# Stating the first two blocks of a lane's next image ahead of the other lane's Fourier and bilinear blocks

## The chip, the cores and the metric

The kernel runs on one core of a Trainium2 chip. It is measured by the device time of one execution in microseconds, as the median of several runs. It is written for a tile framework with a scheduler: the Python code states operations, the framework works out which of them depend on each other, and a scheduler that goes through a simulated timeline fixes, while the program is built, the order in which each engine will execute its own instructions. Where several instructions could go next on an engine, the one stated earlier is preferred. On the chip each engine follows its fixed order, and waits on semaphores for the results of the others.

## The reference

The input x holds 16 images of 56 x 56 positions with 128 channels, in float32. Each image goes through four blocks, each added to its own input:

```python
x = x + L0(_gn(x), ...)   # attention inside shifted 7 x 7 windows, 4 heads
x = x + L1(_gn(x), ...)   # triangle: gated projections, einsum over rows, layer norms
x = x + L2(_gn(x), ...)   # Fourier operators, attention over 56 "time" rows, 32 heads
x = x + L3(_gn(x), ...)   # q, k, v; depthwise 3 x 7 convolutions; three bilinear products
```

Here `_gn` is a group norm with 32 groups of 4 channels. In the Fourier block an image is read as 56 planes of 56 x 128: spectral convolutions that keep a few modes give queries, keys and values, the planes attend to each other, and two more Fourier operators with a GELU between them follow. In the bilinear block

```python
kernel = einsum('xnk,xkd->xnd', q, K_H1)
feature = einsum('xvw,xvd->xwd', V_G, feature)
out = einsum('xnd,xvd->xvn', kernel, feature)
```

is computed at each of the 3,136 positions of an image. Images don't depend on each other.

## The kernel before

An image lies in on-chip memory as 128 channels by 3,136 positions (`xt`). `load_image` (L433) brings it in with 7 loads on SyncE's queue (SP, L439), each followed by 4 transposes on TensorE. Then the four blocks run on it: `_window_attention` (L480), `_triangle` (L615), `_fourier` (L729), `_bilinear` (L1276). The bilinear block writes the result itself, chunk by chunk (L1445), so `store_image` isn't used.

There are two lanes. Image b belongs to lane b % 2, and each lane has its own buffers: one large work area (`arena`, 128 x 17,152 floats), 5 small work tiles (`w2`), 8 tiny ones, 4 banks of PSUM (two single ones, `psb`, and a double one, `psd`), 12 DRAM buffers (`dy`). Each block takes its lane's arena for itself, so inside a lane the blocks run strictly one after the other. The images are in a pool of two buffers that both lanes share, so the next image of a lane can be loaded only once the image before it in the same lane is done. What overlaps is therefore always one image of lane 0 with one image of lane 1.

The blocks differ in what they use. The first two are made of many small matmuls and the evictions of their results, and move almost no data. The Fourier block has an early part (norms, column transforms, attention weights, with the wide products of L1093), a loop over a table (L1188 to L1226: 128 transfers issued by GpSimd at L1200, each read of a table from DRAM multiplied by VectorE at L1202 and summed by TensorE), and a late part (inverse transforms and two operators, with GpSimd clearing buffers at L973, L974 and L1250). The bilinear block writes each of 21 intermediate results to DRAM eight times over (`dy`, L1314, on ScalarE's queue), reads them back spread over the partitions (84 transfers of 448 KB per image, L1408, on SP's queue), multiplies them on VectorE (L1411) and sums the products on TensorE (the helper `together`, L368 and L371).

The order of statements is a plain loop over the images: all four blocks of image 0, then all four of image 1, and so on. So at every moment the scheduler prefers the lane with the older image.

Of the kernel before, what the change touches and what calls it, by code (L numbers as in the profile page):

```python
# [307 lines left out]
def tile_blocks(ctx: ExitStack, tc: tile.TileContext, ins, out, at, stages=(0, 1, 2, 3)):  # L308
    nc = tc.nc
    x_in = ins["x"]  # L310
    NB = x_in.shape[0]
# [16 lines left out]
    lane = [0]  # L328
    count = [0]

    def uid(s):
        count[0] += 1
        return f"{s}{count[0]}"
# [4 lines left out]
    def w2():  # L338
        return w2p[lane[0]].tile([P, 512], F32, tag="w2", name=uid("w2_"))
# [4 lines left out]
    def psb():  # L344
        return ps1[lane[0]].tile([P, 512], F32, tag="ps1", name=uid("psb"))
# [37 lines left out]
    def W(name):  # L383
        rows, o, n = at["wgt"][name]
        return wgt[:rows, o : o + n]
# [47 lines left out]
    def load_image(b):  # L433

        xt = xpool.tile([P, NTOK], F32, tag="xt", name=uid("xt"))
        for q in range(NCH):
            t = w2()
            tv = t[:TT, :].rearrange("p (a c) -> p a c", a=4)
            nc.sync.dma_start(  # L439
                out=tv,  # L440
                in_=xf[b, q * CH : (q + 1) * CH, :].rearrange("(a p) c -> p a c", p=TT),
            )
            p = psb()
            for a in range(4):
                nc.tensor.transpose(p[:, a * TT : (a + 1) * TT], tv[:, a, :], ident[:TT, :TT])
            act(xt[:, q * CH : (q + 1) * CH], p[:, :CH], AF.Identity, bias=W("bout0"))
        return xt

    def store_image(b, xt):
        for q in range(NCH):  # L450
            p = psb()
            for a in range(4):
                o = q * CH + a * TT
                nc.tensor.transpose(p[:TT, a * P : (a + 1) * P], xt[:, o : o + TT], ident)
            t = w2()
            nc.scalar.copy(t[:TT, :], p[:TT, :])
            nc.sync.dma_start(
                out=of[b, q * CH : (q + 1) * CH, :].rearrange("(a p) c -> p a c", p=TT),
                in_=t[:TT, :].rearrange("p (a c) -> p a c", a=4),
            )  # L460
# [1 line left out]
    env = dict(locals())  # L462
    blocks = [_window_attention, _triangle, _fourier, _bilinear]
    run = {s: blocks[s](env) for s in stages}
    for b in range(NB):
        lane[0] = b % 2
        xt = load_image(b)
        done = False
        for s in stages:
            done = run[s](b, xt)  # L470
        if not done:
            store_image(b, xt)


class _Env:
# [1008 lines left out]
def _build(inputs, bacc, stages=(0, 1, 2, 3)):  # L1484
    x = np.ascontiguousarray(inputs["x"])
    w, early, late = _weights({k: v for k, v in inputs.items() if k != "x"})
    arrays, at = {"x": x}, {}
    for name, parts in (("cst", _constants()), ("wgt", w), ("early", early), ("late", late)):
        arrays[name], at[name] = _pack(parts)
    nc = bacc.Bacc("TRN2", target_bir_lowering=False, num_devices=1)  # L1490
    ins = {k: nc.dram_tensor(k, v.shape, F32, kind="ExternalInput").ap() for k, v in arrays.items()}
    out = nc.dram_tensor("out", x.shape, F32, kind="ExternalOutput").ap()
    with tile.TileContext(nc, schedule_with_timeline_sim=True) as tc:
        tile_blocks(tc, ins, out, at, stages)
    return nc, arrays, out, at
```

## Time and profile before

| | |
|---|---|
| runs | 13,435.75, 13,443.8 and 13,488.92 us; median 13,443.8 us |
| profiled execution | 13,405.75 us; span in the profile 13,403.8 us |
| mean TensorE clock granted | 0.847 |
| moved by DMA | 2,106 MB, 157 GB/s over the span |

The profile of this page comes from one execution. Its busy shares say how much of the span an engine executed something. PE is TensorE, PEld its weight loads, DVE is VectorE, ACT ScalarE, POOL GpSimd, SP the queue of SyncE. The three numbers of a wait are the total in us, how often, and the longest. The two costliest groups are the multiplications of the bilinear block and of the table loop, both on VectorE:

```profile
L1411 DVE TENSOR_TENSOR arena<-arena 128x1792 f32<-128x1792 f32 x1344 | 2661.8, 2018 | 724.6 <-DMA arena<-dy 329.5
L1202 DVE TENSOR_TENSOR arena<-arena 112x1344 f32<-112x1344 f32 x1024 | 1569.5, 1552 | 356.8 <-DMA arena<-table 341.1
```

Such a line reads: line and engine, operation, what is written and read with shapes, how many; then busy time and mean nanoseconds of one; then the idle time of the engine ahead of these, and what ended most of it. Since every instruction of an engine stands in the built program in the order in which it runs, the records of VectorE can be paired one by one with the program, and so be told apart by image and block. One image keeps VectorE busy for 82.5 us in the window attention, 67.5 in the triangle, 275 in the Fourier block and 212.5 in the bilinear block.

### The profile page before, as it was taken

How to read it: one execution, taken by the hardware profiler on the slowest of the kernel's cores; microseconds unless marked ns; L12 is line 12 of the kernel's file. 1: busy time of each engine (PE TensorE's matmuls, PEld its weight loads, DVE VectorE, ACT ScalarE, POOL GpSimd, SP SyncE). 2: the span in 40 equal slices, each digit the busy share in tenths (PEclk: the TensorE clock that was granted, in tenths of full speed). 3: DMA queues.
4: the chain of work that ended last, by engine and by line, in shares of the span. 5: the costliest groups of instructions: out<-in, count | busy, mean ns of one | idle time of the engine just before them, and what ended most of it. 6: DMA issues, size and time to landing. Idle time of an engine off the chain costs nothing. (4 is left out here: it accounts for less than half of the span.)

```text
span 13403.8 us, 202422 instructions
## 1 busy us (share of the span) xinstructions
PE 10585.8 (79%) x82624; PEld 5860.7 (44%) x82624; DVE 9623.6 (72%) x13985; ACT 3845.7 (29%) x6638; POOL 1426.4 (11%) x2746
## 2 busy tenths in 40 slices
PE   7887687876878778887778877888778887788776
PEld 4454254542544335443355433554335443354432
DVE  7776868667677686676766667767777677866776
ACT  3223141321423224232242222422224232242221
POOL 0120002200022000220002200022000220002200
PEclk9988898878988889888888778888888888888887
DMA  1256904468044680447804468044780447704577
GB/s 35 73 164 230 315 1 118 118 244 300 1 124 124 237 294 9 118 138 240 276 10 118 131 228 291 13 118 130 245 279 10 118 136 252 270 7 118 131 249 267
DMA packets 1091758, 2105.94 MB, mean 157 GB/s; under 512 B 98320, under 2 KB 974096, under 8 KB 1089680
## 3 DMA queue, kind: packets, MB, share of 16 engines
q1 hardware_dynamic: 560000, 823.95, 18.7%
q0 software_dynamic: 165120, 629.61, 17.1%
q10 hardware_dynamic: 365712, 639.44, 13.2%
q8 instruction: 654, 10.72, 0.3%
q14 instruction: 272, 2.23, 0.1%
HBM read 1412.73 MB, written 667.03 MB: 155 GB/s over the span
## 5 line engine op out<-in xcount | busy, mean ns | idle before, releaser
L1411 DVE TENSOR_TENSOR arena<-arena 128x1792 f32<-128x1792 f32 x1344 | 2661.8, 2018 | 724.6 <-DMA arena<-dy 329.5
L1202 DVE TENSOR_TENSOR arena<-arena 112x1344 f32<-112x1344 f32 x1024 | 1569.5, 1552 | 356.8 <-DMA arena<-table 341.1
L371 PE MATMUL psb<-arena,cst 128*32 128x448 f32 x9792 | 1578.0, 672 | 0.0
L368 PE MATMUL psb<-arena,cst 128*32 128x448 f32 x1408 | 818.8, 670 | 799.9 <-DVE arena L1411 750.3
L1200 POOL DMA_DIRECT2D arena<-table x2048 | 1063.7, 521 | 2799.3 <-PE psb L1116 724.8
L371 PE MATMUL psb<-arena 112*64 112x224 f32 (+2 forms) x4864 | 1245.2, 525 | 0.0
L368 PE MATMUL psb<-arena 112*64 112x448 f32 (+1 forms) x1280 | 691.4, 625 | 369.2 <-DVE arena L1093 187.5
L371 PE MATMUL psd<-arena 112*64 112x224 f32 (+1 forms) x3072 | 749.4, 465 | 0.0
L368 PE MATMUL psd<-arena 112*64 112x448 f32 x1024 | 554.5, 627 | 211.4 <-DVE arena L1202 190.9
L1093 DVE TENSOR_TENSOR arena<-w,coef 128x1792 f32<-128x1792 f32 x256 | 507.6, 2020 | 210.7 <-PE psb L371 187.4
L371 PEld LDWEIGHTS psb<-arena 112*64 112x64 f32 (+1 forms) x4864 | 435.6, 153 | 509.7 <-issue 507.3
L368 PEld LDWEIGHTS psb<-arena,cst 128*32 128x32 f32 x1408 | 118.4, 119 | 1154.3 <-DVE arena L1411 869.2
L678 PE MATMUL psd<-wgt,arena 128*64 128x128 f32 x7168 | 514.4, 293 | 112.4 <-DVE arena L690 96.5
L371 PEld LDWEIGHTS psb<-arena,cst 128*32 128x32 f32 x9792 | 367.6, 125 | 471.4 <-issue 451.0
L1396 ACT COPY arena<-psd 128x896 f32<-128x896 f32 x336 | 303.4, 905 | 930.8 <-DVE arena L1411 549.4
L678 PEld LDWEIGHTS psd<-wgt,arena 128*64 128x64 f32 x7168 | 450.0, 145 | 217.1 <-issue 129.2
L907 PE MATMUL psb<-cst,arena 128*128 128x64 f32 (+1 forms) x2688 | 454.9, 341 | 92.4 <-ACT arena L917 63.2
L371 PE MATMUL psd<-arena,wgt 128*32 128x448 f32 x2688 | 500.6, 604 | 34.4 <-DMA arena<-padded 34.0
L907 PEld LDWEIGHTS psb<-cst,arena 128*128 128x128 f32 x2688 | 437.2, 254 | 148.8 <-ACT arena L917 74.0
L1313 ACT COPY w<-psb 128x448 f32<-128x448 f32 x336 | 178.6, 532 | 1089.1 <-PE psb L371 761.8
L368 PE MATMUL psd<-arena,wgt 128*32 128x448 f32 x896 | 438.6, 607 | 42.4 <-DMA arena<-padded 37.4
L371 PEld LDWEIGHTS psd<-arena 112*64 112x64 f32 x3072 | 287.0, 151 | 284.4 <-issue 283.0
(299 smaller groups left out, 19594.2 us busy)
## 6 DMA issues: line engine op xcount, KB each, us to landing
arena<-table POOLq DMA_DIRECT2D x2048, 294.0 KB, 8.7
dy<-w ACTq DMA_DIRECT2D x336, 1792.0 KB
arena<-dy SPq DMA_DIRECT2D x1344, 448.0 KB
arena<-padded SPq DMA_DIRECT2D x896, 162.8 KB
w<-x SPq DMA_DIRECT2D x112, 224.0 KB
out<-w SPq DMA_DIRECT2D x112, 224.0 KB
padded<-w ACTq DMA_DIRECT2D x336, 62.0 KB
arena<-arena POOLq DMA_DIRECT2D x16, 784.0 KB, 9.8
```

The source lines that it names most:

```text
L368: done = mm(**first)
L371: mm(**kw)
L678: mm(p[half : half + 64, i // 4, i % 4 * P : (i % 4 + 1) * P], lhsT=xh[:, c0 : c0 + 64], rhs=W(w).rearrange("p (k c) -> p k c", c=64)[:, : ...
L907: mm(p[:, 2 * i * nl : 2 * (i + 1) * nl], lhsT=src[:, t * P : (t + 1) * P], rhs=fc, start=True, stop=True)
L1093: tt(t4, bc(ys[c][:, l0 : l0 + 4, :], 1, 8), bc(coef[:, c, h0 : h0 + 8, l0 : l0 + 4], 3, T), ALU.mult,)
L1200: nc.gpsimd.dma_start(out=t[hh * T : (hh + 1) * T, :], in_=bc(tflat[q, two, hh], 0, T))
L1202: tt(t4, bc(x3[:, :, s], 1, 2), t4, ALU.mult)
L1313: nc.scalar.copy(t[:, :CH], p[:, :CH])
L1396: nc.scalar.copy(z, p[:, :, :CH])
L1411: tt(t4, bc(rep, 2, 2), bc(z, 1, 2), ALU.mult)
```

## The change

The four blocks of an image are split in two halves: the first half (`first`) loads the image and runs window attention and triangle; the second half (`second`) runs Fourier and bilinear. The new loop states the second half of image b - 2, then the first half of image b, which is in the same lane. In the new order of statements the first half of image 2 stands after the second half of image 0 and ahead of the second half of image 1, and so on: second(0), first(2), second(1), first(3), second(2), first(4) ... No operation, buffer or size differs.

```diff
-    for b in range(NB):
+    early = [s for s in stages if s < 2]
+    late = [s for s in stages if s >= 2]
+    images = {}
+
+    def first(b):
         lane[0] = b % 2
-        xt = load_image(b)
-        done = False
-        for s in stages:
+        images[b] = load_image(b)
+        for s in early:
+            run[s](b, images[b])
+
+    def second(b):
+        lane[0] = b % 2
+        xt, done = images.pop(b), False
+        for s in late:
             done = run[s](b, xt)
         if not done:
             store_image(b, xt)
+
+    for b in range(NB + 2):
+        if b >= 2:
+            second(b - 2)
+        if b < NB:
+            first(b)
```

## The prediction

> **What bounds the kernel now.** I first read the page's totals, to see whether one engine is full.
>
> ```profile
> PE 10585.8 (79%) x82624; PEld 5860.7 (44%) x82624; DVE 9623.6 (72%) x13985; ACT 3845.7 (29%) x6638; POOL 1426.4 (11%) x2746
> ...
> q1 hardware_dynamic: 560000, 823.95, 18.7%
> q0 software_dynamic: 165120, 629.61, 17.1%
> q10 hardware_dynamic: 365712, 639.44, 13.2%
> ```
>
> None is. Two engines are busy for three quarters of the span each, so what counts is how well two lanes fill each other's gaps. Next, the 40 slices.
>
> ```profile
> DVE  7776868667677686676766667767777677866776
> ...
> POOL 0120002200022000220002200022000220002200
> ...
> DMA  1256904468044680447804468044780447704577
> ```
>
> There is a beat of five slices, 1675 us, which is two images. In each beat there is one slice without DMA: both lanes are then in their first two blocks, which move almost nothing. So the lanes already run almost in step. I then paired the 13,985 recorded VectorE instructions, in order, with those of the built program, whose tile names tell the image. That gives every stage a place in time. Images 2 and 3 start their VectorE work at 1598 and 1667 us, 69 us apart; images 14 and 15 at 11498 and 11710, 212 us apart. Lane 1 is 69, 97, 188, 254, 208, 212, 212 us behind lane 0 in pairs 1 to 7: the lanes drift apart and stay there. The windows view, cut where lane 1 starts an image (and, in its first row, at the end of the span), shows what the drift did to the time of a pair.
>
> ```profile
> 13142.00:13404.00 262.00, 162.56 (x976) 58.10 (x976) 163.73 (x121) 31.76 (x49) 1.01 (x2) 0.76 0.74 252
> 1667.00:3347.00 1680.00, 1330.46 (x10446) 737.92 (x10444) 1208.52 (x1758) 482.00 (x837) 174.22 (x344) 0.85 0.49 156
> 3347.00:5026.00 1679.00, 1329.77 (x10572) 726.64 (x10571) 1221.19 (x1779) 494.13 (x855) 182.23 (x346) 0.86 0.50 156
> 5026.00:6706.00 1680.00, 1327.19 (x10527) 729.30 (x10526) 1207.15 (x1762) 489.98 (x847) 183.54 (x344) 0.86 0.49 156
> 6706.00:8393.00 1687.00, 1343.63 (x10137) 749.40 (x10136) 1184.51 (x1720) 481.86 (x823) 177.37 (x340) 0.82 0.49 155
> 8393.00:10058.00 1665.00, 1327.85 (x10324) 740.91 (x10323) 1197.27 (x1740) 480.96 (x831) 176.41 (x340) 0.84 0.49 157
> 10058.00:11710.00 1652.00, 1329.07 (x10334) 745.44 (x10335) 1197.12 (x1742) 483.15 (x833) 182.67 (x345) 0.85 0.49 159
> ```
>
> After the window and its length come PE, PEld, DVE, ACT, POOL, then PE's clock, DMA share and GB/s. A pair takes 1652 to 1687 us whether the lanes are 69 or 212 us apart. The first row is the end of the span: image 14 is finished at 13142, and lane 1 works alone for 262 us with VectorE busy 62%.
>
> **What the Trainium skill says.** "Perfetto Trace Analysis", section Optimization Strategy, holds that where the contended engine changes between regimes, interleaving the regimes may help. The trace agrees by halves. Per stretch I took the VectorE busy time (mean duration of each line in its stage) over elapsed time. With A the first two blocks, F Fourier, B bilinear: A beside A 0.736, B beside B 0.737, F beside F 0.784; mixed, A beside B 0.861, A beside F 0.788, but B beside F only 0.709. The same page, under Tensor Engine Instruction, calls VectorE, ScalarE and GpSimd strict FIFOs; the one-to-one match of the 13,985 records agrees. So what the scheduler writes down is what runs, and the order of the changed program is evidence of placement. "DMA: Bandwidth & Descriptors", section Issuing engines are not separate DMA queues, says that SP's, ScalarE's and GpSimd's transfers share the same 16 engines; the waits view agrees in kind (SP waits behind ScalarE's transfers):
>
> ```profile
> SPq L1408 <- DMA dy<-w: 1017.8, 136, 284.7
> ...
> DVE arena L1202 <- DMA arena<-table: 341.1, 399, 3.9
> DVE arena L1411 <- DMA arena<-dy: 329.5, 157, 10.5
> ```
>
> **The change part by part.** No instruction is added or removed: 13,985 on VectorE, 43,520 matmul instructions, 2,506 SP transfers, 2,064 GpSimd transfers stand in both programs. What is restated is, per image, 1,088 matmul instructions, 274 on VectorE (82.5 + 67.5 = 150 us), 161 on ScalarE, 22 on GpSimd and 7 loads on SP, counted from the program's stage labels. In statement order image 2's first blocks now precede image 1's Fourier and bilinear, so the scheduler prefers them where both are ready. It cannot pull them far: a lane has one arena and there are two image buffers, so image 2 waits for image 0's last store either way. The same holds for the 7 loads moved past lane 1's reads on SP: in both programs they stand in the second half of lane 1's bilinear reads (image 2's at places 325 to 336 of SP's order before and 317 to 325 after, with image 1's reads ending at 361; image 14's at 2102 to 2122 and 2173 to 2184, with image 13's ending at 2209). I price them at nothing, since a load costs SP 0.43 us to issue and lane 1's repeats run ahead of VectorE in four buffers; SP's waits at the loads sum to 105 us over the whole span, some 7 us for each image, which is what they would cost if that cover were gone. GpSimd's 22 memsets and scalings also stand where they stood, after the other lane's table loads.
>
> What does move is the distance of the lanes. In VectorE's order lane 1's image starts 4, 64, 89, 169, 224, 180, 180, 180 instructions after lane 0's before, and 4, 84, 78, 69, 68, 84, 78, 68 after. The reason follows from the preference: lane 1's first blocks now come ahead of lane 0's Fourier block, so lane 1 catches up in each pair. The change keeps the lanes in step and overlaps unlike stages less, not more. VectorE's busy time by class, before to after: AA 1795 to 2049, BB 1885 to 2677, FF 2878 to 3537, AB 1075 to 517, AF 1259 to 679, BF 1314 to 746 us.
>
> The profile contains such a pair: pair 1, images 2 and 3. Its GpSimd order agrees to 99% with that of pairs 4 and 7 of the changed program, its VectorE order to 79 and 81%; with the other pairs of before VectorE's agrees to 39 to 57%. So I price from it. Lane 1 took 1680 us from image 3 to 5, lane 0 1652 from image 2 to 4; the lag grew by 28 us between, so for a constant lag the middle, 1666, is fairer. The mean of lane 1 over all six pairs is (11710 - 1667)/6 = 1674. I take 1670. The start to 1667 stays (its orders are nearly equal). The last pair is priced as 1679, image 3's own start to end, in place of the 13400 - 11710 = 1690 of image 15. This is the lone tail: after image 14's last instruction lane 1 has 120 VectorE instructions (167 us) before and 37 (66 us) after; 101 us of work at 0.637 instead of 0.737 is 158 - 137 = 21 us saved, and I credit 11. The sum is 1667 + 6 x 1670 + 1679 + 4 (last store) = 13,370 us, against the span of 13,403.8: 34 us less, -0.25%. The profiled execution took 13,405.75, 38 us under the median of 13,443.8; I move the difference over, to 13,410.
>
> **No measurable change, 13,410 us (chance 0.42).** I call within 0.5%, 67 us, what a measurement of this kernel can tell from no change; the three runs themselves spread by 53. Its own range is 13,377 to 13,511.
>
> **Faster, 13,345 us (0.31).** Cutting stages finer (Fourier into its part ahead of the table loop, the loop, and the rest) changes the answer. The worst mixture of before is the early part beside the late part, 983 us at 0.606, and only 142 of its 596 us of work remain so; early beside loop (0.914) rises from 538 to 1049. Loop beside triangle (0.935, 482 us) is lost. Every class at its own rate sums to 13,269 against 13,368, so -99. For it: these rates come from the trace. Against it: pairs 0 and 1 took 1634 and 1680 where the same rates give 1654 and 1659, so the classes' rates are good to about 20 us a pair.
>
> **Slower, bilinear crowding, 13,600 us (0.15).** The place is L1411, waiting for repeats of dy. Two bilinear blocks need (18.7 + 13.2)% x 13,404 / 8 = 534 us of all 16 engines; the slices already read 0.87 DMA share in that stage, and BB rises by 42%. If its rate falls from 0.737 to 0.70, as in pair 7 (305 us in 435, its lone tail included), BB takes 2677/0.70 = 3824 instead of 3632: +192 on the forecast's -34. It decides from a rate of 0.717 down, where the loss passes 0.5%. Against it: pairs 0 and 1, in step, had 0.75.
>
> **Slower, regimes lost, 13,520 us (0.10).** The six coarse classes at their mean rates sum to 13,443 against 13,368, +76, because A beside B at 0.861 is halved. The fine classes speak against it.
>
> **It does what its words say, 12,940 us (0.02).** If every AA stretch (1795 us at 0.736) ran beside another stage at 0.82, 2 x 1795 x (1/0.736 - 1/0.82) = 500 us would go. The order of the changed program excludes this almost wholly: AA grows.
>
> **How the numbers follow.** Faster by over 0.5%: 0.31 + 0.02, less 0.01 for forecasts that land short, 0.32; within 0.5%: 0.42; slower: 0.15 + 0.10, and 0.01 from the forecast's upper edge, 0.26. The range of 13,290 to 13,580 leaves out the last case and the far halves of the fine-class and crowding cases.
>
> **What would show it.** Right: image 15 starts its VectorE work 60 to 120 us after image 14 instead of 212; the two lanes end within some 130 us of each other; pairs take 1655 to 1685 us; busy sums per engine stay within 1%. Crowding shows as more idle time before L1411 put down to dy than 329.5 us, and a DMA share over 0.9 in the bilinear slices; the finer account shows as pairs under 1660. Wrong would be a lag of 200 us in spite of the order, or a pair over 1700 us.

## The result, and the profile after

| | before | after |
|---|---|---|
| median | 13,443.8 us (9 runs, 13,400.9 to 13,499.0) | 13,543.1 us (9 runs, 13,478.6 to 13,587.0) |
| ratio | | 1.0062, 95% interval 1.0036 to 1.0089 |
| profiled execution, span | 13,405.75 us, 13,403.8 us | 13,563.97 us, 13,562.2 us |
| end of lane 1 after lane 0 | 258 us | 88 us |

The changed kernel is slower by 0.6%. The profiled execution of before lies 38 us under its median and that of after 21 us over, so the two profiles differ by 158 us where the medians differ by 99; the sums below are made in the profiles and overstate the loss by that much. Lines of the code from L463 on stand 17 further down in the changed kernel (L1411 is L1428, L1202 is L1219). First the page of the changed kernel, totals and slices:

```profile
PE 10577.3 (78%) x82624; PEld 5842.9 (43%) x82624; DVE 9635.8 (71%) x13985; ACT 3829.1 (28%) x6625; POOL 1424.8 (11%) x2746
...
POOL 0120001200012000120001200012000120001200
...
DMA  1255903559136491264913559034690355904468
```

The sums of busy time are those of before within 0.5%. What differs is the shape: DMA comes in sharper blocks (a 9 in nearly every beat, where before only the first beat has one), since both bilinear blocks now lie beside each other. Next, the groups of instructions by line, VectorE only: busy time and mean, then the idle time ahead and what ended it.

```profile
L1428 DVE TENSOR_TENSOR arena<-arena 128x1792 f32<-128x1792 f32 x1344 | 2650.0, 2018 | 578.1 <-PE psb L371 244.3 <-DMA arena<-dy 223.7 <-ACT arena L1413 81.8
L1219 DVE TENSOR_TENSOR arena<-arena 112x1344 f32<-112x1344 f32 x1024 | 1565.2, 1552 | 400.3 <-DMA arena<-table 388.5 <-issue 3.2 <-PE psd L371 3.0
```

In spite of the sharper blocks VectorE waits less for the repeats of `dy` than before (223.7 us against 329.5), and 47 us more for the table. Last, the windows of the changed kernel, cut where lane 1 starts images 3, 5, 7, 9, 11, 13, 15, and its lone end:

```profile
1742.00:3444.00 1702.00, 1331.02 (x10290) 737.47 (x10289) 1196.72 (x1734) 475.65 (x823) 180.64 (x338) 0.84 0.49 154
3444.00:5161.00 1717.00, 1337.52 (x10292) 737.27 (x10292) 1197.42 (x1739) 479.50 (x828) 176.31 (x343) 0.83 0.49 153
5161.00:6845.00 1684.00, 1308.42 (x10311) 718.65 (x10299) 1198.46 (x1741) 479.62 (x830) 179.25 (x345) 0.85 0.49 156
6845.00:8500.00 1655.00, 1319.23 (x10436) 732.09 (x10438) 1206.40 (x1750) 481.71 (x836) 175.92 (x347) 0.85 0.49 159
8500.00:10194.00 1694.00, 1317.46 (x10297) 732.66 (x10294) 1196.77 (x1735) 476.59 (x824) 180.02 (x340) 0.84 0.49 155
10194.00:11892.00 1698.00, 1321.62 (x10253) 734.12 (x10251) 1197.53 (x1736) 477.82 (x826) 178.60 (x340) 0.84 0.49 154
13471.00:13562.00 91.00, 48.93 (x312) 14.80 (x312) 63.55 (x37) 7.88 (x12) 0.00 (x0) 0.73 0.68 227
```

A pair takes 1692 us on average (before 1674), with the same work of VectorE in it. The lanes stay 75 to 95 us apart from pair 1 to the end, as the order said; two pairs took over 1700 us, which the prediction had named as a sign that it is wrong. The lone end has shrunk to 91 us. Image 3 starts at 1742 instead of 1667. So, from the span of before: +75 for the first pair, 6 x 18 = +108 for the pairs, -24 for the last (1666 instead of 1690): +159, the whole difference of the profiles. Lane 1 is counted here because it ends the span.

### The profile page after: what moved, and what is told of

It reads as the page before. It is cut to its first block, busy times and chain, and to the rows that moved or that the text cites. A ratio compares the mean times of both kernels' runs of the same rounds, so it can differ in the third digit from the quotient of the medians.

```text
span 13562.2 us, 202398 instructions
## 1 busy us (share of the span) xinstructions
PE 10577.3 (78%) x82624; PEld 5842.9 (43%) x82624; DVE 9635.8 (71%) x13985; ACT 3829.1 (28%) x6625; POOL 1424.8 (11%) x2746
## 5 line engine op out<-in xcount | busy, mean ns | idle before, releaser
L1428 DVE TENSOR_TENSOR arena<-arena 128x1792 f32<-128x1792 f32 x1344 | 2650.0, 2018 | 578.1 <-PE psb L371 244.3
L1219 DVE TENSOR_TENSOR arena<-arena 112x1344 f32<-112x1344 f32 x1024 | 1565.2, 1552 | 400.3 <-DMA arena<-table 388.5
L371 PE MATMUL psd<-arena 112*64 112x224 f32 (+1 forms) x3072 | 788.8, 487 | 0.0
L368 PE MATMUL psd<-arena 112*64 112x448 f32 x1024 | 584.0, 657 | 249.7 <-DVE arena L1219 222.5
L962 PE MATMUL psd<-cst,arena 112*32 112x112 f32 x8960 | 366.8, 289 | 126.5 <-ACT w L969 107.7
```

The costliest lines, as they stand in the source:

```text
L368: done = mm(**first)
L371: mm(**kw)
L962: mm(o, lhsT=half[:, 32 * k + 8 * g + 4 * u + i, :], rhs=C(f"di{c + 1}"), start=c == 0, stop=c == last)
L1219: tt(t4, bc(x3[:, :, s], 1, 2), t4, ALU.mult)
L1428: tt(t4, bc(rep, 2, 2), bc(z, 1, 2), ALU.mult)
```

## The experiments

Times of pairs in what follows are found as in the prediction, from VectorE's records paired with the program; the mean of a kernel is that of lane 1 over pairs 1 to 6, in one profiled execution. That execution lay up to 82 us (10 us a pair) from the median of its kernel's runs, so differences of this size between kernels say little. "Distance" is by how many us lane 1 starts an image after lane 0. Ratios are to the kernel before, run on the same chip in the same sitting. The expectations name their theories by letters: S and D (later S2 and D2) say that the distance of the lanes decides, O and P that the preference does, U that the mixture of stages hardly matters, A that each loss belongs to the statement order in its place, N that every order is a draw.

**Is it the distance, or the preference? A cut elsewhere.** Two kernels differ from the changed one in where the blocks are cut.

```diff
-    early = [s for s in stages if s < 2]
-    late = [s for s in stages if s >= 2]
+    early = [s for s in stages if s < 1]
+    late = [s for s in stages if s >= 1]
```

> Only the load and the window attention of the next image are stated ahead (the cut is at s < 1); triangle, Fourier and bilinear stay in the second half. In VectorE's order lane 1 then starts its images 64, 84, 162, 170, 181, 202, 184 instructions after lane 0, almost as in the kernel before (64 to 224) and unlike the changed one (68 to 84). Theory S (the distance of the lanes sets the time): as the kernel before, ratio 0.997 to 1.003, pairs of 1650 to 1690 us. Theory O (what costs is that first blocks are preferred over the other lane's second half, whatever the distance): some of the 1.006 stays, 1.003 or more. Theory N (every reordering throws the dice anew, the distance has no part in it): anything from 0.99 to 1.01.

Measured: ratio 1.0021 (1.0004 to 1.0038); distances of 70 to 220 us, pairs of 1657 to 1712 us, mean 1689. The ratio stays inside the bound that S set, close to before, but three of the six pairs lie over S's 1690, and in the profile they are hardly better than those of the changed kernel. O's bound (1.003 or more) isn't excluded by this run. The other cut is at `s < 3`:

> Window attention, triangle and Fourier of the next image are stated ahead (s < 3), only bilinear stays behind. VectorE's order has the lanes 69, 120, 117, 117, 117, 120, 125 instructions apart: between the changed kernel (68 to 84) and before (64 to 224). Theory S: between the two, ratio 1.002 to 1.006, lanes 100 to 150 us apart. Theory O: as bad as the changed kernel or worse, 1.006 or more, since more is preferred. Theory N: anything from 0.99 to 1.01.

Measured: ratio 0.988 (0.9844 to 0.9916), median 13,279.0 us; distances of 133 to 149 us from image 4 on, pairs of 1640 to 1670 us, mean 1655. Every theory missed this: S, because it isn't between before and after; O, because more is preferred and it is faster; N's lower bound was 0.99. O falls here.

**Lanes far apart.** Image 1's loads are made to wait for image 0 by a copy into the load's own work tile. For the statement order of before:

```diff
         xt = xpool.tile([P, NTOK], F32, tag="xt", name=uid("xt"))
+        held.setdefault(b, xt)
...
             t = w2()
+            if b == 1:
+                nc.vector.tensor_copy(t[:TT, 0:1], held[0][:TT, 0:1])
```

> Statement order of the kernel before, but the loads of image 1 wait for image 0's Fourier block (a one-column copy into the load's work tile reads image 0 first; the load then overwrites it). In VectorE's order the lanes are then 1261, 1208, 1151, 1083, 1057, 1028, 985 instructions apart, over half a pair (some 870 of 1745). The wait costs some 800 us once, at the start or as a longer lone end. Theory S: unlike stages lie side by side, so pairs take 1560 to 1620 us and win back 50 to 110 us each, the total being 1.00 to 1.03. Theory U (the mixture of stages hardly matters, the two engines' sums do): pairs stay at 1650 to 1700 us and the total is 1.04 to 1.06.

Measured: ratio 1.0537 (1.0502 to 1.0572); distances of 1059 to 1273 us; pairs of 1641 to 1718 us, mean 1678. The lanes draw together in this kernel, so lane 1 alone is too favourable: the mean of both lanes is 1696. The same edit on the statement order of the change:

> Statement order of the changed kernel, but the loads of image 1 wait for image 0's triangle in the same way. In VectorE's order the lanes are 656, 717, 718, 718, 719, 733, 718 instructions apart, first blocks beside the other lane's second half. The wait costs 300 to 400 us once. Theory S: pairs of 1560 to 1620 us, the total 0.97 to 1.00. Theory U: pairs of 1680 to 1710 us as in the changed kernel, the total 1.02 to 1.04.

Measured: ratio 1.0249 (1.0214 to 1.0284); distances of 591 to 623 us; pairs of 1663 to 1696 us, mean 1681. Two pairs of this kernel in the windows view:

```profile
3828.00:5510.00 1682.00, 1295.74 (x10328) 715.05 (x10328) 1196.26 (x1742) 507.45 (x850) 176.65 (x342) 0.86 0.50 156
5510.00:7206.00 1696.00, 1311.83 (x10352) 724.41 (x10353) 1196.62 (x1742) 507.09 (x850) 177.30 (x342) 0.85 0.50 155
```

Here the stages that lie side by side are nearly always unlike ones, and a pair still takes what it took. Both ratios lie in the ranges of theory U: mixing the stages wins nothing in these two kernels. S in its first form, that a larger distance is better, falls with it.

**Small shifts at the start.** A copy of one column marks the moment at which image 0 is through a row of windows, and image 1's loads wait for it (eight tiny VectorE copies in all, not the two that the first expectation says). The expectations forgot that this wait itself costs time: it delays lane 1's start by 77 or 139 us, and in all four runs the ratios that the theories of distance and preference gave were missed as they stand. What is left of a ratio when the whole delay is taken off is an estimate.

```diff
+            if b == 1:
+                nc.vector.tensor_copy(t[:TT, 0:1], gate[:TT, 0:1])
...
+            if b == 0 and wi == 1:
+                nc.vector.tensor_copy(e.gate, dst[:, 0, 0, 0:1])
```

> Statement order of the changed kernel; image 1's loads wait for image 0's second window row (two one-element copies more). In VectorE's order the lanes are 81, 97, 68, 78, 78, 78, 69, 68 instructions apart: the same distance as in the changed kernel, another fine order. Theory S2 (lanes less than 100 us apart meet in the same thin stretches of triangle and Fourier): as slow as the changed kernel, 1.004 to 1.009. Theory P (the preference itself costs): the same. Theory N (the fine order is drawn anew each time): 0.985 to 1.015, and not tied to 1.006.

Measured: ratio 1.016 (1.0117 to 1.0203). The delay is 77 us (0.57%), which leaves 1.010. Distances of 74 to 114 us, pairs mean 1695, against 1692 in the changed kernel: another fine order at the same distance, the same time of a pair.

> Statement order of the changed kernel; image 1's loads wait for image 0's fifth window row. In VectorE's order the lanes are 132, 221, 221, 226, 226, 226, 226, 226 instructions apart, as far as in the kernel before (180 to 224 in its later pairs). Theory S2: the loss goes, 0.998 to 1.003, and triangle beside triangle almost vanishes. Theory P: 1.004 to 1.009 as in the changed kernel. Theory N: no tie to either.

Measured: ratio 1.0167 (1.0122 to 1.0212); less the delay of 139 us (1.03%) 1.006, as in the changed kernel. Distances of 253 to 261 us, pairs mean 1685. Triangle beside triangle shrank from about 1,000 us to 25, and still 11 of the 18 us a pair stay: S2's "the loss goes" isn't met. The seven us gained are less than one profile can tell, as this one lay 64 us under the median.

> Three blocks stated ahead, as in the run that took 0.988, with image 1's loads waiting for image 0's fifth window row. In VectorE's order the lanes are 132, 221, 181, 163, 197, 221, 190, 221 instructions apart instead of 117 to 125. Theory S2 (0.988 came from a distance of 135 us): about as the kernel before, 0.996 to 1.003. Theory P (stating three blocks ahead is good by itself): 0.985 to 0.992. Theory N: no tie to either.

Measured: ratio 1.013 (1.0092 to 1.0168), less the same delay 1.003. Distances of 189 to 258 us, pairs mean 1684, although three blocks are stated ahead. P falls: the same preference that gave 1655 gives 1684 at another distance.

> Statement order of the kernel before; image 1's loads wait for image 0's second window row. In VectorE's order the lanes are 81, 165, 183, 221, 184, 220, 220, 226 instructions apart from the start on, where before they drifted to 180 by the third pair. Theory S2: 0.996 to 1.002, since the distance hardly changes. Theory P: 0.998 to 1.002. Theory N: a spread of the size of 1.006 or 0.988 shows here too.

Measured: ratio 1.0106 (1.0073 to 1.0139), less a delay of 77 us 1.005. Distances of 184 to 261 us, pairs mean 1685, where the kernel before took 1674 at 187 to 254. So 1674 is itself on the good side of what the orders at this distance gave.

**Half of the change.** First the new order for images 0 and 1 alone:

```diff
-    for b in range(NB + 2):
-        if b >= 2:
-            second(b - 2)
-        if b < NB:
-            first(b)
+    for b in range(2):
+        first(b)
+    for b in range(2):
+        second(b)
+    for b in range(2, NB):
+        first(b)
+        second(b)
```

> Only the first pair is stated in the manner of the change (both first halves, then both second halves); from image 2 on the order of statements is that of the kernel before. VectorE's order has the lanes 4, 84, 169, 220, 221, 199, 226, 220 instructions apart. In the profiles image 3 began 75 us later in the changed kernel than before, and its pairs then took 1692 us instead of 1674. Theory A (both losses belong to the statement order that stands there): image 3 begins near 1742 us, later pairs take 1674, ratio 1.003 to 1.006. Theory N (every order is a draw, pairs of 1655 to 1695 whatever the statement order): later pairs near 1685, ratio 1.004 to 1.013.

Measured: ratio 1.0073 (1.0037 to 1.0109). Image 3 starts at 1714 us; distances grow to 262 us; pairs mean 1683, as N expected. The reverse keeps images 0 and 1 as before (`first(b)` and `second(b)` for each) and enters the new loop at image 2:

> The reverse: images 0 and 1 stated as before, the new order of statements from image 2 on. VectorE's order has the lanes 4, 64, 86, 86, 78, 86, 86, 86 instructions apart. Theory A: image 3 begins near 1667 us, later pairs take 1692 as in the changed kernel, the end saves some 24 us; ratio 1.001 to 1.006. Theory N: later pairs anywhere from 1655 to 1700, ratio 0.988 to 1.008.

Measured: ratio 1.0132 (1.0096 to 1.0168), median 13,549.2 us. Image 3 starts at 1661 us; distances of 69 to 98 us; pairs mean 1691. Two of its pairs:

```profile
1661.00:3376.00 1715.00, 1348.05 (x10454) 744.22 (x10451) 1210.39 (x1757) 485.49 (x840) 183.40 (x344) 0.84 0.49 153
3376.00:5079.00 1703.00, 1325.05 (x10331) 733.68 (x10330) 1203.20 (x1742) 481.39 (x831) 181.76 (x342) 0.85 0.49 154
```

In the profiles theory A holds for the start (1714 and 1661) and for the later pairs of the second kernel (1691). In the first kernel the later pairs didn't return to 1674, both ratios lie above A's range of 1.006, and they don't add up to that of the change.

**Other orders, chosen for their distance.** Block by block for each pair of images:

```diff
+    for b in range(0, NB, 2):
+        for s in range(4):
+            for i in (b, b + 1):
...
+                run[s](i, images[i])
```

> The two images of a pair are stated block by block: both window attentions, both triangles, both Fourier, both bilinear blocks. VectorE's order has the lanes 4, 87, 73, 86, 84, 84, 84, 84 instructions apart, the distance of the changed kernel with another preference. Theory D (lanes under 100 us apart lose some 10 us a pair against lanes 200 us apart): pairs of 1685 to 1700 us, ratio 1.004 to 1.010. Theory N: pairs anywhere from 1655 to 1700, ratio 0.988 to 1.010.

Measured: ratio 1.0104 (1.0064 to 1.0144); distances of 93 to 98 us, pairs mean 1689. A third statement order near 85 us, and the same time once more. Then, per pair, `first(b)`, `first(b + 1)`, `second(b + 1)`, `second(b)`:

> Both first halves of a pair, then lane 1's second half ahead of lane 0's. VectorE's order has the lanes only 4, 1, 45, 46, 45, 62, 45, 49 instructions apart. Theory D: worse than the changed kernel, pairs over 1700 us, ratio 1.008 or more, with triangle beside triangle and Fourier's early part beside its late part at 0.4 to 0.6. Theory N: pairs anywhere from 1655 to 1700, ratio 0.988 to 1.010.

Measured: ratio 0.9988 (0.9962 to 1.0013); distances of 1 to 62 us, mostly 43 to 45; pairs mean 1673, in a profile 82 us over the median. D in this form falls: closer than the changed kernel, and as fast as before.

Four more were to tell a rule of distance from chance. The three-block cut from image 2 on, with images 0 and 1 stated as before:

> Images 0 and 1 stated as before, from image 2 on three blocks stated ahead. VectorE's order has the lanes 4, 64, 76, 120, 117, 117, 117, 120 instructions apart, the distance of the run that took 0.988. Theory D2 (distance decides: bad near 85 us, good near 135): later pairs of 1645 to 1665 us, ratio 0.985 to 0.993. Theory N (each order is a draw): pairs anywhere from 1655 to 1700, ratio 0.988 to 1.010.

Measured: ratio 0.9854 (0.9808 to 0.99), median 13,258.3 us, the fastest of all. Its pairs 1 and 3 (the pair of images 0 and 1 is pair 0), in the windows view:

```profile
1666.00:3363.00 1697.00, 1341.35 (x10415) 732.12 (x10414) 1205.13 (x1750) 481.52 (x832) 179.47 (x342) 0.84 0.50 155
5021.00:6672.00 1651.00, 1295.88 (x10328) 716.88 (x10328) 1198.58 (x1741) 478.38 (x828) 181.82 (x342) 0.86 0.50 159
```

D2's ranges are met, and within one kernel the pair in which the lanes are 72 to 88 us apart takes 1697 us, and one in which they are 131 to 134 apart takes 1651. PE's busy time fell too, with a clock of 0.86 instead of 0.84.

> Per pair of images: three blocks of both, then both bilinear blocks. VectorE's order has the lanes 4, 69, 109, 164, 201, 251, 184, 132 instructions apart. Theory D2: the pairs at 109 to 132 instructions near 1655 us, those at 164 to 251 near 1683, ratio 0.995 to 1.003. Theory P (three blocks ahead is good by itself): ratio 0.985 to 0.992. Theory N: no tie of a pair's time to its distance.

Measured (three blocks of both images of a pair, then both bilinear blocks): ratio 0.9989 (0.9966 to 1.0012); distances from 81 to 280 us, pairs mean 1681. P is refuted again. D2's ratio is met, but its tie of single pairs can't be read here, because in every pair the distance changes by 44 us or more.

> All four blocks of an image are stated together as before, but the lanes take turns in being first (0, 1, 3, 2, 4, 5, 7, 6 ...). VectorE's order has the lanes -1 to 4 instructions apart in every pair: fully in step. Theory D2 makes no forecast below 45 us; a plain rule that being in step is bad gives pairs over 1700 us and 1.010 or more. Theory N: pairs anywhere from 1655 to 1700.

Measured (the lanes take turns in going first): ratio 0.9992 (0.9973 to 1.0011); distances of 0 to 2 us, pairs mean 1678. Being fully in step costs nothing that shows.

> Per pair: three blocks of both images, then lane 1's bilinear block ahead of lane 0's. VectorE's order has the lanes 4, 63, 62, 62, 62, 65, 62, 62 instructions apart. Theory D2: between the 45 us run (1673) and the 85 us runs (1692), pairs of 1675 to 1695, ratio 0.999 to 1.008. Theory P: 0.985 to 0.992. Theory N: pairs anywhere from 1655 to 1700.

Measured: ratio 0.991 (0.988 to 0.9941); distances of 61 to 72 us, pairs mean 1666. D2 expected 1675 to 1695 and missed: if there is a bad stretch, it begins above 72 us. P's range, 0.985 to 0.992, is met: this kernel too states three blocks ahead.

**All profiles together.** Of the 18 kernels I took those pairs (1 to 6) in which the distance changed by no more than 25 us, and the mean of both lanes' start-to-start time (the spread is the standard deviation):

| distance, us | pairs | kernels | us per pair, mean and spread |
|---|---|---|---|
| 0 to 5 | 6 | 1 | 1678, 16 |
| 20 to 58 | 5 | 1 | 1671, 22 |
| 58 to 73 | 6 | 1 | 1666, 7 |
| 73 to 100 | 24 | 6 | 1691, 19 |
| 100 to 150 | 9 | 2 | 1648, 8 |
| 150 to 240 | 6 | 2 | 1675, 23 |
| 240 to 290 | 11 | 3 | 1679, 15 |
| 500 to 700 | 6 | 1 | 1680, 9 |
| over 1000 | 3 | 1 | 1693, 29 |

Between 73 and 100 us, where the change puts the lanes, pairs are slowest but for three pairs far apart, and just beyond they are fastest. This is no rule of distance yet. 22 of the 24 pairs come from four kernels (means of 1687 to 1698), and the kernels near 255 us, at 1685 in two cases, are no more than a profile's error away. The good values at 58 to 73 and at 100 to 150 us come from three kernels that all state three blocks ahead, so distance and preference aren't separated there by a run. Against the preference alone stand the two kernels with the same preference at other distances, 1684 and 1681, and the pair of 1697 above.

Between 73 and 100 us the time goes with something finer. The traces give for each how long one lane's early Fourier part (ahead of the table loop) lay beside the other's late part. In 20 pairs it was 55 to 67 us, and they took 1668 to 1726, mean 1696; in four it was 20 to 25 us, and they took 1645 to 1689, mean 1667.

## Why the prediction was wrong

**What was right.** The reading of the order. The change doesn't do what its words say: the lanes come closer (75 to 95 us apart, forecast 60 to 120), the ends lie 88 us apart (forecast within some 130), busy sums agree within 1%, and the last image took 1666 us where 1679 was forecast. The seven loads, priced at nothing, cost nothing: SP waited at them for 79 us in the span, less than the 105 of before. Crowding in the bilinear blocks, the first slower rival, showed one of its two signs, a DMA share of 0.9 in the slices, but it didn't cost: bilinear beside bilinear ran at about 0.75, no worse than 0.737, and waits for `dy` fell. One line doesn't carry what the prediction shows it for: SP's 1017.8 us behind `dy<-w` are reads of repeats (L1408) that wait until these repeats are written (L1314), and would stand there if the queues shared nothing. No run here shows the sharing.

**The step that failed** is the price of a pair: "So I price from it ... I take 1670." Measured: 1692, 130 us more over six pairs. The order had told me which pairs of the changed program resemble pair 1: pairs 4 and 7. Those took 1655 and 1666. I gave the same price to the other five, whose order doesn't resemble it, and they took 1702, 1717, 1684, 1694 and 1698. The statement under it, that a pair takes the same "whether the lanes are 69 or 212 us apart", rested at the near end on one or two pairs. That pairs 4 and 7 came in near the price is in part luck: pair 1 of the kernel with only the later order changed (1715) and of the fastest kernel (1697), both shown above, agree with pair 1 of before on VectorE and GpSimd as closely as pairs 4 and 7 do (85 and 90% of VectorE's built order in matching stretches, against 84% for each of these), and took 35 and 17 us longer than its 1680.

The second term was "The start to 1667 stays (its orders are nearly equal)": 1742 instead. Of these 75 us, lane 1 lost 33 up to the end of its table loop, 37 in the late Fourier part of image 1 and 5 in its bilinear block. The kernel with only the start changed has the same order as the changed one on every engine until image 2 begins, and tells which part repeats. Its late part is as long (301 us, against 298 in the changed kernel and 261 before), but its loop ended only 10 us later than before. The late part in the windows view, before, after, and with only the start changed:

```profile
871.00:1132.00 261.00, 209.62 (x1741) 144.95 (x1744) 183.27 (x430) 123.78 (x220) 10.87 (x20) 0.76 0.13 44
```

```profile
904.00:1202.00 298.00, 235.63 (x1868) 157.75 (x1869) 195.86 (x447) 134.84 (x233) 10.89 (x20) 0.76 0.19 65
```

```profile
881.00:1182.00 301.00, 239.59 (x1871) 160.99 (x1871) 196.14 (x446) 135.17 (x233) 12.12 (x22) 0.76 0.19 65
```

So one built order gave 1742 in one execution and 1714 in another. Four kernels that share the start of before lie at 1661 to 1681: the loss goes with the order, its size is known to some 30 us, and why the late part takes longer stays open.

**The rivals.** The coarse account, "regimes lost", gave 13,520 us and came nearest to 13,543, at a chance of 0.10. Its reason isn't borne out, so that is luck: with the lanes 600 or 1100 us apart nearly all stretches are mixed, and pairs take 1680 and 1696 us (mean of both lanes). "Perfetto Trace Analysis" of the Trainium skill, section Optimization Strategy, says that interleaving regimes may help; in this kernel those two runs show no gain from it. The fine account (faster, 13,345) failed because a class's rate (VectorE's work over elapsed time) isn't a property of the class. Early Fourier beside late Fourier ran at 0.61 before and at 0.36 after, triangle beside triangle at 0.71 and 0.61: a rate changes with the parts of the two stages that meet. One such meeting in the changed kernel, images 10 and 11, by the windows, the waits and VectorE's timeline:

```profile
9187.00:9254.00 67.00, 59.52 (x432) 42.73 (x428) 23.66 (x24) 30.66 (x51) 6.06 (x12) 0.82 0.24 58
```

```profile
DVE sm L1194 <- PE psb L1192: 16.6, 1, 16.6
DVE arena L1182 <- DMA arena<-arena: 9.4, 1, 9.4
```

```profile
9223.12 1.81 DVE L1190 TENSOR_REDUCE sm<-arena 112x56 f32<-112x896 f32 x1
9241.54 0.15 DVE L1194 COPY sm<-psb 56x1 f32<-56x1 f32 x1 [16.61 <-PE psb L1192]
9241.81 0.27 DVE L1198 SCALAR_TENSOR_TENSOR sm<-psb,sm,cst 56x56 f32<-56x56 f32 x1
```

For 67 us PE is busy 89% and VectorE 35%. VectorE's next step is one column of lane 1 (L1194), and the tiny matmul that it needs (L1192) stands in PE's order behind other groups. In the wait of 16.6 us PE's timeline shows about 10 us of lane 1's own products (L1176), overlapping with some 8 of lane 0's transposes and products (L1252, L1257), which have no work for VectorE in them. Each of the five slow pairs has some 65 us of this class, pairs 4 and 7 have 25. That this meeting is what makes those pairs slow is read from the traces and wasn't tried by itself. All waits at L1194 sum to 88 us in the changed kernel and to 47 before (L1177 there), so that they explain a quarter of the 158 at most. The two pairs named above, of 1715 and 1697 us, have only 28 and 25 us of the class, so it isn't the whole. And the kernel with the lanes 135 us apart spends more time in the same class, at 0.69.

## What to carry to other kernels

With a scheduler between statement and chip, a change of statement order is first a draw of a new fine order: 16 variants with the same work, up to eight tiny copies, spread over 1655 to 1695 us a pair, so look at several orders before giving one a reason, and try the neighbours (here the cut one block further on, 1.2% faster than before, and 1.5% with the first two images stated as before). Don't price a new order with one stretch of the old profile: take every stretch of its kind. Even where the order agrees closely, one stretch was a single draw here (1655, 1697 and 1715 us for orders like that of a pair that took 1680). A mean rate for "stage beside stage" isn't a price either, since here it changed with the parts of the stages that met.

## What the hardware showed unasked

The granted TensorE clock differs with the order. The two kernels with the three-block cut at 135 us had 0.858 and 0.856 and spent 10,395 us of busy time on the matmuls for which the kernel before, at 0.847, needed 10,586 (first of the two); the kernel with the lanes furthest apart had 0.826. The tie to the time is loose: the kernel with only the later order changed had 0.852 in its profile, and ran 1.3% longer than before. Whether the clock makes the order faster or the order the clock isn't shown by these runs.
